# Rotary low parts in one subtraction, high parts copied by ScalarE in portions, and one block of values moved behind the first output products

## The chip, the core and the metric

The kernel runs on one core of a Trainium2 chip. The core has five engines with a queue of instructions each: TensorE (PE, matrix products; PEld is its loading of weights), VectorE (DVE), ScalarE (ACT), GpSimd (POOL) and SyncE (SP, which here only issues DMAs). The metric is the device time of one execution in microseconds, as the median of the runs. Products write PSUM, which has eight banks of 128 partitions by 512 fp32 numbers; all other tiles of the kernel lie in SBUF.

## The reference

One layer: attention with low-rank projections (MLA) over 2048 tokens of width 512, a layer norm, a linear layer, and a second layer norm.

```python
cq = rms_norm(hidden_states @ w_qa.T, q_a_ln_w)               # 384 wide
q = (cq @ w_qb.T)                                             # 16 heads of 192
q_nope, q_pe = (q[..., :128], q[..., 128:])
q_pe = q_pe * cos + rotate_half(q_pe) * sin
ckv = hidden_states @ w_kva.T                                 # 128 + 64 wide
k_pe = k_pe * cos + rotate_half(k_pe) * sin                   # one for all heads
kv = (rms_norm(ckv[..., :128]) @ w_kvb.T)                     # k_nope and v of each head
scores = einsum('bhqd,bhkd->bhqk', q_full, k_full) * scale    # causal
attn = softmax(scores)
out = einsum('bhqk,bhkd->bhqd', attn, v) @ w_o.T
x = layernorm(x + out)
x = layernorm(x + (x @ (weight * scale_weight).T + bias))
```

## The kernel before

**Numbers in two parts.** An operand of a product is held as a high part, rounded to TensorE's fp32r format, and a low part, the remainder. A product is then three products (high by high, high by low, low by high). `split` (L61) makes the two parts: ACT rounds, DVE subtracts.

**Tiles and stages.** The 2048 queries are cut into four blocks of 512 (`b`), the 16 heads into eight pairs (`p`). A block has four query tiles of 128 (`qt`), so that a pair has eight steps in a block (head `j` of query tile `qt`), counted 2 * qt + j from 0 to 7. Block 0 has short rows and runs beside the preparation of keys, values and weights. Blocks 1 to 3 run in `units` (L615) one after the other, with rows up to 1024, 1536 and 2048 keys long. In the trace block 1 runs from about 260 us, block 2 from about 505, block 3 from about 860 to 1332. Then come the output products and both layer norms.

**One step.** `head_scores` (L421) lets PE form the scores of one head and one query tile (L410, products of `Kn` by `qn` and of `Kp` by `pe`), DVE takes the maximum (L448) and makes the bias, ACT takes the exponential (L463, `pr`). `head_probs` (L479) runs a step later: ACT makes the high half of the probabilities (L484, `hl`), DVE the low half (L487), and SP issues the DMA that transposes both into a ring (L491). `values` (L529) multiplies them by V on PE (L540, tile `o`) up to `lag` query tiles later, in two halves; ACT empties `o` into `ot` (L545), and SP stores `ot`.

**PSUM in the blocks.** Two banks (pool `m`) turn among `o`, the projections `ps_qn` and `ps_pe`; a third tile of them waits until the first is emptied by ACT or DVE. The other six banks hold scores. In block 1 they are three tiles of two banks, one tile for each head. In block 2 each head has one tile of two banks and one of one bank, two of each kind. In block 3 each head has two tiles of two banks, and three such tiles turn.

**Projections as fillers.** The queries of the next pair are projected between the steps of this one. `project_nope` (L369) makes `qn` for a pair; `project_pe` (L324) makes `pe`, the rotary part for four heads (a group `g`, two pairs), so it runs at every other pair. Each is a generator, and `fill` (L551) resumes the first of the list `fillers` up to its next `yield`. The tuple `at` in `units` says at which of the eight steps `fill` is called.

`project_pe` has PE form two tiles `ps_pe`, DVE multiplies them by cosine and sine into `prod` (L341), and POOL adds and subtracts, which leaves the rotated numbers in `rp`, 128 partitions by two rows of 512 (L348, L349). ACT rounds them to `ph` (L351). Then the eight pieces of 32 partitions are stacked so that each head has its high parts in partitions 0 to 63 of `pe` and its low parts in 64 to 127. In block 0 and in the first group of block 1 (`quick`), ACT copies the high parts (L360) and DVE, partly POOL, subtracts the low ones. In the other eleven groups POOL does both (L362 and L363).

**Who sets the order.** In blocks 1 to 3 PE and SP follow the program text. ACT, DVE and POOL are ordered by the scheduler of the build, except that from the second query tile of block 3 on ACT and DVE follow the text too (L646). In the text, a head's high and low probabilities stand inside the next head's step, behind that step's first scores.

**The end of the attention.** After the last step two query tiles of values are still to come, `o3_7_2` (15 key tiles, halves of 21 and 24 products) and `o3_7_3`. The loop at L803 mixes the halves of the first with the output products of the first two pairs (`accumulate`, L753, into four PSUM accumulators `accs`, one bank each) and with `value_output` (L173), which multiplies V's weights by the output weights for later pairs. The accumulators take banks that the scores held.

Of the kernel before, what the change touches and what calls it, by code (L numbers as in the profile page):

```python
# [11 lines left out]
F32 = mybir.dt.float32  # L12
F32R = mybir.dt.float32r
AF = mybir.ActivationFunctionType
ALU = mybir.AluOpType
# [4 lines left out]
P = 128  # L20
# [5 lines left out]
NB = 4  # L26
QB = 512
# [22 lines left out]
def mla_block(ctx: ExitStack, tc: tile.TileContext, a, out):  # L50
    nc = tc.nc
# [59 lines left out]
    blk = ctx.enter_context(tc.tile_pool(name="blk", bufs=2, side="right"))  # L111
# [168 lines left out]
    state = {"queue": nc.gpsimd}  # L280
# [43 lines left out]
    def project_pe(b, g, direct=None):  # L324

        if direct is None and ("wpe", b, g) not in state:
            load_wpe(b, g)
        w = state.pop(("wpe", b, g)) if direct is None else direct
        cq, cs = state["cq"], state["cs"]
        prod = prj.tile([P, 2, 2, QB], F32, tag="prod", name=f"prod{b}_{g}")  # L330
        for x in range(2):
            ps = psum["m"].tile([P, QB], F32, tag="m", name=f"ps_pe{b}_{g}_{x}")
            n = 0
            for lt in range(LT):
                for i, k in ((0, 0), (0, 1), (1, 0)):
                    nc.tensor.matmul(  # L336
                        ps, w[:, i, lt, x * P : (x + 1) * P], cq[:, k, lt, :], start=n == 0, stop=n == 8
                    )
                    n += 1
            for k in range(2):  # L340
                nc.vector.tensor_tensor(prod[:, k, x, :], ps, cs[:, k ^ x, :], ALU.mult)  # L341
            if x == 0:
                yield
            elif b or g == 3:
                load_wpe(*((b, g + 1) if g < 3 else (b + 1, 0)))
        rp, tp = prod[:, 0], prod[:, 1]
        eng = nc.vector if (b, g) == (0, 0) else nc.gpsimd
        eng.tensor_tensor(rp[:, 0, :], rp[:, 0, :], rp[:, 1, :], ALU.subtract)  # L348
        eng.tensor_tensor(rp[:, 1, :], tp[:, 0, :], tp[:, 1, :], ALU.add)  # L349
        ph = prj.tile([P, 2, QB], F32R, tag="ph", name=f"ph{b}_{g}")  # L350
        nc.scalar.activation(ph, rp, AF.Copy)  # L351
        pe = blk.tile([P, 4, QB], F32R, tag="pe", name=f"pe{b}_{g}")

        quick = b == 0 or (b, g) == (1, 0)
        for j in range(4):
            q = slice(32 * j, 32 * j + 32)
            for x in range(2):
                to = pe[32 * x : 32 * x + 32, j, :]
                if quick:
                    nc.scalar.activation(to, rp[q, x, :], AF.Copy)  # L360
                else:
                    nc.gpsimd.tensor_copy(to, rp[q, x, :])  # L362
                (nc.gpsimd if not quick or (b, g) == (0, 0) and j % 2 else nc.vector).tensor_tensor(  # L363
                    pe[64 + 32 * x : 96 + 32 * x, j, :], rp[q, x, :], ph[q, x, :].bitcast(F32), ALU.subtract
                )
        state["pe", b, g] = pe
        yield

    def project_nope(b, p, direct=None):  # L369
# [181 lines left out]
    def fill(n=1):  # L551
        while n > 0 and fillers:
            try:
                next(fillers[0])
                n -= 1
            except StopIteration:
                fillers.pop(0)
# [57 lines left out]
    def units(pool, ring, b):  # L615
        lag = min(ring.shape[1] // (2048 * (b + 1)) - 1, 3)

        for p in range(NPAIR):
            put_in(True)


            if p + 1 == NPAIR:
                at = (1, 2, 4, 5) if b < NB - 1 else (1, 3, 5, 7)
            elif p % 2 == 0 and p + 2 < NPAIR:
                at = (0, 1, 2, 3) if (b, p) == (1, 0) else (0, 1, 3, 4)
            else:
                at = (3, 4)
            if b and p % 2 == 0 and p + 2 < NPAIR:
                fillers.append(project_pe(b, p // 2 + 1))
            if p + 1 < NPAIR:  # L630
                fillers.append(project(b, p + 1) if b == 0 else project_nope(b, p + 1))
            elif b + 1 < NB:
                fillers.append(project(b + 1, 0))
            if b == NB - 1 and p == NPAIR - 1:
                ctx_p.close()
                pcr = state["pcr"] = ctx.enter_context(
                    tc.tile_pool(name="pcr", bufs=2, side="right", reuse_waits="tile")
                )
                state["wvo"] = [pcr.tile([P, 2, 2, HID], F32R, name=f"wvo{p}", bufs=1) for p in range(EARLY)]
                for i in range(EARLY):  # L640
                    fillers.append(value_output(i, psum["m"], "m"))
                at = (3, 4, 5, 6)
            for qt in range(4):
                nk = (4 * b + qt + 1) * P
                if (b, p, qt) == (NB - 1, 0, 1):
                    ctx_f.enter_context(tc.manual_schedule(engines={ET.PE, ET.SP, ET.DVE, ET.Activation}))  # L646
                if (b, p, qt) == (0, NPAIR - 1, 3):
                    s0, PT = -4 * nk, prj.tile([P, 4 * nk], F16, tag="ph", name="carry")
                else:
                    s0 = room(2048 * (b + 1), ring.shape[1], 4 * nk, (b, p) == (2, NPAIR - 1) and qt > 0)  # L650
                    PT = ring[:, s0 : s0 + 4 * nk]
                vg = values(b, p, qt, nk, PT)
                if nk <= 512:
                    pi = pair_scores(pool, b, p, qt, nk)
                    flush()
                    probs.append(pair_probs(pool, b, p, qt, nk, PT, *pi))
                    fill()
                    next(side[0], None)
                    if p and qt % 2:
                        next(side[1], None)  # L660
                    if qt % 2:
                        next(side[0], None)
                    run_values(lag)
                    run_values(lag)
                else:
                    for j in range(2):
                        prepare_output(b, p, 2 * qt + j)
                        prev = probs.pop() if probs else iter(())
                        pi = head_scores(pool, b, p, j, qt, nk, prev)
                        probs.append(head_probs(pool, b, p, j, qt, nk, PT, *pi))  # L670
                        if (b, p, qt, j) == (1, 0, 1, 0):
                            half_values()
                            half_values()
                        if 2 * qt + j in at:
                            fill()
                        run_values(lag)
                vals.append([vg, 0, s0, s0 + 4 * nk])
            drain()
        if b:
            flush()  # L680
# [102 lines left out]
    with tc.manual_schedule(engines={ET.PE, ET.SP}), ExitStack() as ctx_f:  # L783
        for b in range(1, NB):
            with ExitStack() as ctx_s:
                for k in ("s", "ts", "us")[b - 1]:
                    psum[k] = ctx_s.enter_context(
                        tc.tile_pool(name=f"ps_{k}{b}", bufs=1, space=PSUM, reuse_waits="tile")
                    )
                pools = [  # L790
                    ctx_s.enter_context(tc.tile_pool(name=f"{k}{b}", bufs=2, reuse_waits="tile")) for k in ("hl", "pr")
                ]
                units(pools, ring, b)

        ps_a = ctx.enter_context(tc.tile_pool(name="ps_a", bufs=4, space=PSUM, reuse_waits="tile"))
        accs = [ps_a.tile([P, HID], F32, tag="acc", name=f"acc0_{t}") for t in range(4)]
        pcq = ctx.enter_context(tc.tile_pool(name="pcq", bufs=1, side="right", reuse_waits="tile"))
        wvo = state["wvo"]
        wvo += [pcq.tile([P, 2, 2, HID], F32R, name=f"wvo{EARLY + i}") for i in range(2)]
        load_wo(2, blk, "pe")  # L800
        latent_load(0, EARLY + 1)
        load_wo(3, blk, "qn")
        for p in range(EARLY):  # L803
            vo = value_output(EARLY + p, psum["m"], "m")
            for t in range(4):
                if len(vals) > 1:
                    half_values()
                accumulate(accs[t], p, t, *cuts[0, p])
                if t in (1 - p, 2 - p):
                    next(vo)  # L810
            cuts[0, EARLY + p] = latent_split(0, EARLY + p)
        while vals:
            half_values()
        put_in(True)
# [160 lines left out]
```

## Time and profile before

| what | value |
|---|---|
| time, median of 3 runs | 1597.79 us (1594.83 to 1601.57) |
| the profiled execution | 1599.18 us, its span 1597.4 us |
| PE matrix products, busy | 1550.6 us, 97% |
| PE idle from 290 to 1332 us | 8.3 us of 1042 |
| PE's longest single wait, at 1337.70 us | 3.56 us, for the DMA that transposes `hl` |
| L463 exponentials, ACT | 324.6 us in 320 |
| L484 high probabilities, ACT | 294.5 us in 320 |
| L487 low probabilities, DVE | 359.4 us in 320 |
| L363 low rotary parts, POOL | 140.4 us in 92, 1526 ns each |
| L362 high rotary parts, POOL | 66.8 us in 88, 760 ns each |
| mean granted TensorE clock | 0.992 of full speed |

The span goes from the first instruction to the last; the profiled execution's own time holds 1.8 us more. A row of the profile names a source line, an engine and an operation, then what it writes and reads, then how many there were and how long one took. "[1.44 <-ACT ot L545]" behind a row of a timeline says that the engine stood idle for 1.44 us before it, and that the eviction of line 545 on ACT ended the wait. An idle engine costs time only if the chain that ends last passes through it.

### The profile page before, as it was taken

The numbers are of one execution on the slowest core, as the hardware profiler recorded it, in microseconds if no ns is written. First come the engines' busy times: TensorE is split into PE (matmuls) and PEld (weight loads), VectorE is DVE, ScalarE is ACT, GpSimd is POOL, SyncE is SP. The second block draws the span as 40 slices with busy tenths as digits, with TensorE's granted clock in tenths as the row PEclk, the third lists the DMA queues.
The fourth block names the chain that finished last, engine by engine and source line by source line (L and its number), as shares of the span: only waits on it lengthen the run. The fifth ranks groups of instructions, "written<-read, shape, count | busy, mean of one in ns | idle before, by whom it ended". The sixth has DMA issues, their size and how long they took to land. (4 is left out here: it accounts for less than half of the span.)

```text
span 1597.4 us, 24700 instructions
## 1 busy us (share of the span) xinstructions
PE 1550.6 (97%) x9130; PEld 1293.8 (81%) x9130; DVE 1164.0 (73%) x2099; ACT 926.1 (58%) x1631; POOL 364.6 (23%) x434
## 2 busy tenths in 40 slices
PE   8898998999999999999999999999999998999997
PEld 7777877888888788888888888888888886788886
DVE  6777777888787878787787777777777775455564
ACT  5767676666665766767765665665666665321120
POOL 2333234252206305050022400400400000022132
PEclk9999999999999999999999999999999999999999
DMA  6888667789897987888896888878678798433230
GB/s 210 255 211 223 173 187 163 163 165 184 166 208 159 180 158 165 164 160 168 154 222 137 165 146 168 157 144 168 137 144 170 155 230 190 145 112 129 92 113 33
DMA packets 633032, 262.49 MB, mean 164 GB/s; under 512 B 570288, under 2 KB 611376, under 8 KB 631888
## 3 DMA queue, kind: packets, MB, share of 16 engines
q1 hardware_dynamic: 621472, 233.62, 68.1%
q0 software_dynamic: 4672, 17.73, 3.6%
q10 hardware_dynamic: 6768, 9.57, 2.1%
q8 instruction: 72, 1.18, 0.3%
q14 instruction: 48, 0.39, 0.1%
HBM read 83.17 MB, written 35.13 MB: 74 GB/s over the span
## 5 line engine op out<-in xcount | busy, mean ns | idle before, releaser
L410 PE MATMUL s<-Kn,qn 128*128 128x512 f32 (+4 forms) x1920 | 519.5, 376 | 6.2 <-ACT pr L463 4.4
L463 ACT ACTIVATE pr<-s,bias,rq 128x1024 f32<-128x1024 f32 (+3 forms) x320 | 324.6, 1018 | 215.0 <-DVE bias L457 157.9
L540 PE MATMUL o<-ring,V 128*128 128x256 f16 x3252 | 395.5, 274 | 12.2 <-DMA ring<-hl 5.2
L487 DVE SCALAR_TENSOR_TENSOR hl<-pr,inv,hl 128x1024 f16<-128x1024 f32 (+7 forms) x320 | 359.4, 1136 | 40.0 <-ACT hl L484 35.2
L410 PEld LDWEIGHTS s<-Kn,qn 128*128 128x128 f32 x1920 | 338.6, 190 | 52.9 <-ACT pr L463 7.8
L540 PEld LDWEIGHTS <-V 128*128 128x128 f16 x3264 | 303.7, 98 | 92.5 <-issue 52.8
L410 PE MATMUL s<-Kp,pe 128*128 128x512 f32 (+4 forms) x1280 | 360.4, 362 | 0.0
L484 ACT ACTIVATE hl<-pr,inv 128x1024 f16<-128x1024 f32 (+7 forms) x320 | 294.5, 961 | 92.6 <-issue 34.4
L448 DVE TENSOR_REDUCE neg<-s 128x1 f32<-128x1024 f32 (+3 forms) x320 | 317.8, 993 | 37.3 <-PE s L410 34.2
L410 PEld LDWEIGHTS s<-Kp,pe 128*128 128x128 f32 x1280 | 233.1, 188 | 29.6
L348 POOL TENSOR_TENSOR prod<-prod 128x512 f32<-128x512 f32 x15 | 19.3, 1288 | 641.9 <-DVE prod L341 641.9
L380 PE MATMUL ps_qn<-cq,wq 128*128 128x512 f32 x576 | 147.0, 400 | 4.1 <-ACT ot L545 3.3
L757 PE MATMUL acc<-wvo,oh 128*128 128x512 f32 x448 | 144.2, 403 | 0.0
L363 POOL TENSOR_TENSOR pe<-prod,ph 32x512 fp32r<-32x512 f32 x92 | 140.4, 1526 | 11.0 <-issue 5.1
L380 PEld LDWEIGHTS ps_qn<-cq,wq 128*128 128x128 f32 x576 | 108.3, 192 | 25.9 <-ACT ot L545 3.9
L757 PEld LDWEIGHTS acc<-wvo,oh 128*128 128x128 f32 x448 | 83.6, 189 | 21.2 <-issue 3.8
L475 DVE TENSOR_SCALAR inv<-sums 128x1 f32<-128x1 f32 x128 | 27.0, 211 | 98.6 <-ACT pr L463 98.5
L757 PE MATMUL acc<-wvo,ol 128*128 128x512 f32 x224 | 88.2, 394 | 0.0
L336 PE MATMUL ps_pe<-cq,wpe 128*128 128x512 f32 x288 | 71.9, 395 | 1.5 <-DMA cq<-cq_d 1.4
L545 ACT ACTIVATE ot<-o 128x256 f32<-128x256 f32 x128 | 48.4, 379 | 40.9 <-PE o L540 37.1
L362 POOL CAST pe<-prod 32x512 fp32r<-32x512 f32 x88 | 66.8, 760 | 3.3
L64 ACT ACTIVATE oh<-o 128x1024 fp32r<-128x1024 f32 x28 | 29.7, 1061 | 65.1 <-PE acc L757 51.8
(140 smaller groups left out, 1586.1 us busy)
## 6 DMA issues: line engine op xcount, KB each, us to landing
wq<-wq_d SPq DMA_DIRECT2D x22, 768.0 KB, 5.7
o<-ot_d SPq DMA_DIRECT2D x32, 512.0 KB, 3.3
ot_d<-ot SPq DMA_DIRECT2D x97, 128.0 KB, 2.3
wpe<-wpe_d SPq DMA_DIRECT2D x10, 768.0 KB, 5.4
wq<-wq_d POOLq DMA_DIRECT2D x9, 768.0 KB, 6.4
wq_d<-wst SPq DMA_DIRECT2D x9, 512.0 KB, 4.4
cq_d<-cqst SPq DMA_DIRECT2D x18, 256.0 KB, 3.5
wo<-in_wo_dram SPq DMA_DIRECT2D x4, 1024.0 KB, 6.2
```

The lines of the kernel that those rows point to most:

```text
L336: nc.tensor.matmul(ps, w[:, i, lt, x * P : (x + 1) * P], cq[:, k, lt, :], start=n == 0, stop=n == 8)
L362: nc.gpsimd.tensor_copy(to, rp[q, x, :])
L363: (nc.gpsimd if not quick or (b, g) == (0, 0) and j % 2 else nc.vector).tensor_tensor(pe[64 + 32 * x : 96 + 32 * x, j, :], rp[q, x, :], ph ...
L380: nc.tensor.matmul(ps, w[:, i, lt, j * P : (j + 1) * P], cq[:, k, lt, :], start=n == 0, stop=n == 8)
L410: nc.tensor.matmul(ps[:, :w], lhs, K[:, i, c0 : c0 + w], start=n == 0, stop=n == 4)
L448: nc.vector.tensor_reduce(neg[:, ti : ti + 1], v, axis=AX.XY, op=ALU.max, negate=True)
L463: nc.scalar.activation(pr[:, c0 : c0 + n * w].rearrange("p (a c) -> p a c", a=n), v, AF.Exp, bias=bias, scale=r, accum_out=sums[:, ti : ti ...
L484: nc.scalar.activation(hl[:, 0, c], pr[:, c], AF.Copy, scale=inv)
L487: nc.vector.scalar_tensor_tensor(hl[:, 1, c], pr[:, c], inv, hl[:, 0, c], ALU.mult, ALU.subtract)
L540: nc.tensor.matmul(ps[:, :256], vt[:, i, k % 4, :], v[:, :, l, k, :], start=n == 0, stop=n == 3 * kts - 1)
L545: nc.scalar.activation(ot, ps[:, :256], AF.Copy)
L757: nc.tensor.matmul(acc, l[:, t, c], state["wvo"][p][:, i, j, :], start=p == 0 and j == 0 and n == 0, stop=p == NPAIR - 1 and j == 1 and n ...
```

## The change

It has three parts.

1. In the eleven groups that are not `quick`, the eight subtractions of 32 partitions on POOL become one of 128 partitions by 1024 numbers, from `rp` and `ph` into the second half of `prod` (`pl`), and POOL copies the eight low pieces from there. The eight high pieces are copied by ACT.
2. The group's work is issued in more steps: a `yield` stands ahead of `ph`, and the copies are a generator of their own (`stack`), which yields after the first and the third of its four pieces and goes to the end of `fillers`. The tuples `at` have seven entries in place of four, so that PE's projections come at the same steps as before, `ph` and the first two high copies one step later than before, and the other high copies at the last two entries.
3. At the end, the first half of `o3_7_2` is issued behind all of the first pair's output products, and its second half behind the first tile of the second pair's; the steps of `value_output` move with them.

```diff
         rp, tp = prod[:, 0], prod[:, 1]
+        quick = b == 0 or (b, g) == (1, 0)
         eng = nc.vector if (b, g) == (0, 0) else nc.gpsimd
         eng.tensor_tensor(rp[:, 0, :], rp[:, 0, :], rp[:, 1, :], ALU.subtract)
         eng.tensor_tensor(rp[:, 1, :], tp[:, 0, :], tp[:, 1, :], ALU.add)
+        if not quick:
+            yield
         ph = prj.tile([P, 2, QB], F32R, tag="ph", name=f"ph{b}_{g}")
         nc.scalar.activation(ph, rp, AF.Copy)
-        pe = blk.tile([P, 4, QB], F32R, tag="pe", name=f"pe{b}_{g}")
-
-        quick = b == 0 or (b, g) == (1, 0)
-        for j in range(4):
-            q = slice(32 * j, 32 * j + 32)
-            for x in range(2):
-                to = pe[32 * x : 32 * x + 32, j, :]
-                if quick:
-                    nc.scalar.activation(to, rp[q, x, :], AF.Copy)
-                else:
-                    nc.gpsimd.tensor_copy(to, rp[q, x, :])
-                (nc.gpsimd if not quick or (b, g) == (0, 0) and j % 2 else nc.vector).tensor_tensor(
-                    pe[64 + 32 * x : 96 + 32 * x, j, :], rp[q, x, :], ph[q, x, :].bitcast(F32), ALU.subtract
-                )
-        state["pe", b, g] = pe
+        pe = state["pe", b, g] = blk.tile([P, 4, QB], F32R, tag="pe", name=f"pe{b}_{g}")
+
+        if not quick:
+            pl = tp.bitcast(F32R)
+            nc.gpsimd.tensor_tensor(pl, rp, ph.bitcast(F32), ALU.subtract)
+
+        def stack():
+            for j in range(4):
+                q = slice(32 * j, 32 * j + 32)
+                for x in range(2):
+                    hi, lo = pe[32 * x : 32 * x + 32, j, :], pe[64 + 32 * x : 96 + 32 * x, j, :]
+                    nc.scalar.activation(hi, rp[q, x, :], AF.Copy)
+                    if not quick:
+                        nc.gpsimd.tensor_copy(lo, pl[q, x, :])
+                    else:
+                        (nc.gpsimd if (b, g) == (0, 0) and j % 2 else nc.vector).tensor_tensor(
+                            lo, rp[q, x, :], ph[q, x, :].bitcast(F32), ALU.subtract
+                        )
+                if not quick and j in (0, 2):
+                    yield
+
+        rest = stack()
+        if quick:
+            for _ in rest:
+                pass
+        else:
+            next(rest)
+            fillers.append(rest)
         yield
...
             if p + 1 == NPAIR:
-                at = (1, 2, 4, 5) if b < NB - 1 else (1, 3, 5, 7)
+                at = (1, 2, 3, 4, 5, 6, 7) if b < NB - 1 else (1, 3, 5, 7)
             elif p % 2 == 0 and p + 2 < NPAIR:
-                at = (0, 1, 2, 3) if (b, p) == (1, 0) else (0, 1, 3, 4)
+                at = (0, 1, 1, 2, 3, 4, 5) if (b, p) == (1, 0) else (0, 1, 2, 3, 4, 5, 6)
             else:
                 at = (3, 4)
...
-                        if 2 * qt + j in at:
-                            fill()
+                        fill(at.count(2 * qt + j))
                         run_values(lag)
...
         for p in range(EARLY):
             vo = value_output(EARLY + p, psum["m"], "m")
             for t in range(4):
-                if len(vals) > 1:
+                if p and len(vals) > 1:
                     half_values()
                 accumulate(accs[t], p, t, *cuts[0, p])
-                if t in (1 - p, 2 - p):
+                if t in (1, 2):
                     next(vo)
```

## The prediction

> **What bounds the kernel now.** I read the busy shares first, then the busy time by stretch, then what TensorE waited for inside the attention blocks, then the timelines around each of those waits.
>
> ```profile
> PE 1550.6 (97%) x9130; PEld 1293.8 (81%) x9130; DVE 1164.0 (73%) x2099; ACT 926.1 (58%) x1631; POOL 364.6 (23%) x434
> ```
>
> ```profile
> 290.00:560.00 270.00, 264.83 (x1614) 223.81 (x1612) 221.28 (x458) 174.26 (x285) 83.11 (x73) 1.00 0.88 176
> 560.00:900.00 340.00, 338.89 (x2068) 285.06 (x2067) 271.58 (x494) 226.00 (x400) 83.92 (x72) 1.00 0.82 165
> 900.00:1332.00 432.00, 429.96 (x2622) 356.54 (x2621) 323.54 (x465) 275.18 (x404) 42.84 (x36) 1.00 0.81 161
> ```
>
> The columns are stretch, length, then busy time of PE, weight loads, DVE, ACT and POOL. From 290 to 1332 us PE lacks only 5.2 + 1.1 + 2.0 = 8.3 us. The change leaves PE's own order untouched up to there (it only renumbers which fill step issues a projection), so a gain inside the attention blocks is capped at that, while a loss is not: any wait put on PE goes straight to the end. Nearly all the idle time lies beside a rotary group, at 293.6 (0.58), 296.1 (0.52), 489.2 (0.71), 499.8 (0.63), 526.4 (1.44), 530.0 (1.20), 878.2 (0.92), 884.9 (0.19), 1004.3 (0.38) and 1124.2 us (0.38). I call the eleven changed groups by block and number, (1,1) to (3,3).
>
> **POOL's part.** Per group POOL does two adds of 1.29 us, eight casts (about 6.4 us) and eight subtractions (about 12.6 us).
>
> ```profile
> L363 POOL TENSOR_TENSOR pe<-prod,ph x92: 1262/1294/2115, 44.7 to 1135.9; 32x512 fp32r<-32x512 f32 x92
> L362 POOL CAST pe<-prod x88: 602/609/1475, 272.3 to 1124.3; 32x512 fp32r<-32x512 f32 x88
> L360 ACT ACTIVATE pe<-prod x40: 612/628/633, 41.0 to 255.7; 32x512 fp32r<-32x512 f32 x40
> ```
>
> After: one subtraction of 128x1024. A POOL pass over 512 elements takes 1.29 us on 128 partitions (the adds) as on 32, so 2.6 us; then eight low copies, 6.4 us, as the casts now. POOL falls by 12.6 - 2.6 = 10 us a group. That is worth nothing by itself: PE waits for POOL nowhere in its list, and a group is read a pair later or more. Bounds: zero and zero, even if the subtraction took twice as long.
>
> It helps DVE, which POOL slows. The low half of a probability row, 128x640, with POOL idle and during POOL's subtractions (two of them):
>
> ```profile
> 358.56 0.89 DVE L487 SCALAR_TENSOR_TENSOR hl<-pr,inv,hl 128x640 f16<-128x640 f32 x1
> 524.27 3.73 DVE L487 SCALAR_TENSOR_TENSOR hl<-pr,inv,hl 128x640 f16<-128x640 f32 x2 [2.10 <-ACT hl L484]
> ```
>
> 0.89 against 1.87 us each. The Trainium skill ("SBUF — State Buffer", Who interferes with whom) speaks against a wide instruction here: a VectorE instruction with two SBUF inputs and a GpSimd one that reads SBUF share a port, whichever starts first holds it for the whole instruction, and the other is blocked. By the rule one 2.6 us subtraction can hold one DVE instruction for 2.6 us instead of 1.3. By the row, about five such DVE instructions a group lose 1 us each. Either way DVE loses at most 2.6 us at once, then only the smaller loss beside copies (1.34 us in place of 0.89 at 329.7), so DVE gains some 2 us a group. This ends waits that DVE causes: I take 0.6 of the 1.10 at (1,1), the 0.63 at (2,0) and the 1.20 at (2,1); in block 3 the late ph moves a head on, which ends 0.19 + 0.38 + 0.38 = 0.95. The 0.92 at 878.2 stays: that head's ACT waited for a transpose.
>
> **ACT's part: blocks 1 and 2.** Eight high copies per group at 0.64 us (four in a row take 2.56 in block 0) add 5.1 us to ACT. The fill steps would spread them over later heads, but in blocks 1 and 2 the scheduler orders ACT itself: in the built program all eight stand around ph, as four, ph, four, with at most a probability row between. ACT runs in order, so exponentials and evictions queue behind 6.1 us where 1.06 stood. Each group is replayed with the durations of its rows, overlaps of about 0.1 us taken off. Group (1,2):
>
> ```profile
> 327.75 1.29 POOL L348 TENSOR_TENSOR prod<-prod 128x512 f32<-128x512 f32 x1 [36.78 <-DVE prod L341]
> 331.40 0.98 ACT L463 ACTIVATE pr<-s,bias,rq 128x768 f32<-128x768 f32 x1
> 336.01 0.38 ACT L545 ACTIVATE ot<-o 128x256 f32<-128x256 f32 x1
> 336.39 2.23 PE L380 MATMUL ps_qn<-cq,wq 128*128 128x512 f32 x9
> ```
>
> ps_qn takes the PSUM buffer that ot empties, with no slack: 336.01 + 0.38. After: the copies can begin at 329.0 (first POOL add done), 331.6, row 332.3, ph 333.3, copies 335.9, exponential 336.8, qn 337.4, exponential 338.4, ot 338.8. PE waits **2.4 us**. (1,3) is the same picture with the row ahead: ot at 398.6, wanted at 396.44, **2.2**. (3,0): the copies start at 829.05 behind the exponentials; +5.1 +1.0, row 836.6, exponentials 838.3, ot 838.7, wanted at 836.88 by the next o: **1.8**. (2,0): ps_qn waits for DVE's qn, which comes 1.2 us late instead of 0.71: +0.5, less the 0.63, **-0.1**. (2,1): the exponential of the next head but one now ends at 523.6 and its score buffer was wanted at 521.51, a wait of 2.2 where 2.64 stood, **-0.4**. (1,1) **-0.6**. (2,2), (2,3): ot at 615.0 against 615.8 wanted: **0**. Sum **+5.3**; bounds -3.6 (all waits of before but the DMA one gone, no new one) and +10 (each of the eight pays 1.2 more than the mean).
>
> **ACT's part: block 3.** ACT and DVE stand in program order, so the portions do land later: ph and two copies, then four, then two. The first finds room (projection heads). The last two fall in the longest rows, where a loop runs with almost no slack: exponential, high half on ACT, low half on DVE, maximum, bias, next exponential.
>
> ```profile
> 1028.93 2.08 ACT L484 ACTIVATE hl<-pr,inv 128x960 f16<-128x960 f32 x2 [0.26 <-ACT ot L545]
> 1030.06 1.22 DVE L487 SCALAR_TENSOR_TENSOR hl<-pr,inv,hl 128x960 f16<-128x960 f32 x1
> 1032.82 1.21 ACT L463 ACTIVATE pr<-s,bias,rq 128x1024 f32<-128x1024 f32 x1 [1.80 <-DVE bias L457]
> 1035.51 0.86 PE L410 MATMUL s<-Kn,qn 128*128 128x512 f32 x3
> ```
>
> The first of ACT's two halves ends near 1030.0, DVE starts on it at once, and PE's scores at 1035.51 need the buffer of the exponential that ends at 1034.03: 1.4 us of slack. Four copies put this hl off by 2.56 less about 0.3 of waiting it hides: 2.2. Two more before the next row: 1.28 - 0.53, in all 2.95. The third head has 0.6 of slack (exponential to 1048.0, scores at 1048.72), so PE loses 2.95 - 0.6 = **2.3 us** a group; 3 x 2.3 = 6.9, less the 0.95 above: **+5.9**. Bounds -1.0 (slack I don't see) and +8.
>
> **The end.** Before, PE reached the values last but one at 1334.14 and waited for their transpose:
>
> ```profile
> 1337.70 3.60 PE L540 MATMUL o<-ring,V 128*128 128x256 f16 x21 [3.56 <-DMA ring<-hl]
> 1340.94 1.20 PE L757 MATMUL acc<-wvo,oh 128*128 128x512 f32 x2
> ```
>
> ```profile
> 1338.00:1342.00 4.00, 4.00 (x23) 3.11 (x22) 2.27 (x4) 2.86 (x5) 0.00 (x0) 0.60 1.06 200
> ```
>
> The granted clock is 0.60 behind it: 21 products take 3.24 us (2.22 at 1023.8), the six of acc 2.08 (1.39 later); so 3.56 + 1.7. After, the first pair's products stand first. The PSUM addresses of the build put accumulator 0 in the buffer freed by the exponential at 1330.3, but 1 and 2 in that of the last head's first exponential, 1335.92 + 1.21. So six products (1.39) run, then PE waits from 1335.53 to 1337.26: 1.73. Then wo products and the rest; the values want DVE's low half of wo, behind the last rows until 1343.3: 0.2. Saved 5.26 - 1.93 = **3.3 us**. Is PE cold after 1.73? The skill ("TensorE: Matmul & The Clock Gate", Part 1) has the clock halve after an idle window of about 3.4 us; the row at 526.40 shows nine products at 2.36 us behind an idle 1.44. By both warm; by the one cold row, 1.6. On SP one load of o now goes ahead of a 128 KB store; that store is late with its values and nobody at hand waits for it. Bounds 1.5 to 3.6.
>
> **Sum.** +5.3 + 5.9 - 3.3 = +7.9 us on the profiled execution's 1599.18 (span 1597.4), which is 1.4 above the median of the runs. On the median: 1597.8 + 7.9 = **1605.7**.
>
> **Rivals.** *Relief wins (faster):* the scores and evictions turn out to have 2 us more slack than I read, no copy reaches PE, and 6.0 us of the old waits go too, with 3.3 at the end: 1588.5; with half the waits, 1592. For it: ACT is busy 64% of blocks 1 to 3. Against it: ps_qn at 336.39 starts the moment its buffer is free. It decides if ot in (1,2) is ready by its old time. *ACT becomes the bound:* every block 1 and 2 group stops PE by most of its 5.1 us less 2 of slack: 8 x 3.1 + 5.9 - 3.3 = +27, 1625. For it: the block of 6.1 us is longer than the slack of any head replayed. Against: (2,2) and (2,3) have 0.8 to spare after all of it. *Blocks 1 and 2 as read, block 3 with slack:* 5.3 - 1.0 - 3.3 = +1, 1599. *The spreading is not done* in blocks 1 and 2 is not a rival but part of the forecast.
>
> **How the numbers follow.** 0.5% is 8 us, what a measurement of this kernel can tell from none. My case (+3 to +12) 0.66; block 3 with slack (-1 to +3) 0.10; relief wins 0.13; ACT the bound 0.11. My case lies across the line: half of it over 8. Slower 0.33 + 0.11 = 0.44; faster 0.06 (less than half of the relief case reaches 8); same 0.50. Low end: the sum of the low bounds, -3.6 - 1.0 - 3.3, is -8; I stop at -3. High end +14, into the third case.
>
> **What would show it.** ACT's rows of 32x512: 128 in place of 40, near 0.63. PE waits for ot near 336 and 396, for exponentials in the long rows of block 3 (2.3 a group), and 1.7 in place of 3.56 at 1334, at full clock. DVE rows near 524 under 1.4 us. PE's idle time from 290 to 1332 near 19 us; if below 8, ACT had slack that I didn't see and the forecast is wrong.

## The result, and the profile after

The changed kernel takes 1619.12 us, the median of 4 runs (1617.41 to 1624.14), against 1598.01 for the kernel before in the same runs: a ratio of 1.0132 with a 95% interval of 1.0102 to 1.0161. It is slower by 21.1 us, where 7.9 were forecast, and lies outside the range of 1595 to 1612. The profiled execution is the slowest of the four: 1624.14 us, span 1622.4, 25.0 above the profiled execution of before.

The first part of the page, busy time of each engine:

```profile
PE 1559.7 (96%) x9130; PEld 1297.7 (80%) x9130; DVE 1143.7 (70%) x2099; ACT 978.1 (60%) x1719; POOL 253.5 (16%) x357
```

POOL lost 111 us and ACT gained 52, as the change says. TensorE does the same 9130 products, yet is busy 9.1 us longer: part of the loss is not idle time. The same three stretches as before, at the times at which the same products now run (columns as before; the last but two is the granted clock):

```profile
295.00:576.00 281.00, 269.30 (x1618) 226.72 (x1618) 215.14 (x458) 193.39 (x317) 43.85 (x44) 0.99 0.86 171
576.00:920.00 344.00, 339.95 (x2065) 285.79 (x2065) 263.09 (x496) 242.22 (x428) 41.96 (x44) 1.00 0.82 163
920.00:1359.00 439.00, 431.84 (x2624) 356.34 (x2622) 319.46 (x465) 288.41 (x423) 22.73 (x22) 1.00 0.80 158
```

PE's idle time in them is 11.7 + 4.1 + 7.2 = 22.9 us (8.3 before, 19 forecast), and its busy time rose by 7.4. The rows that replace those of the subtractions, by shape:

```profile
L366 ACT ACTIVATE pe<-prod 32x512 fp32r<-32x512 f32 x128 | 80.4, 628 | 4.7 <-POOL prod L349 2.8 <-DVE prod L349 0.3
L368 POOL CAST pe<-prod 32x512 fp32r<-32x512 f32 x88 | 62.9, 714 | 4.6
...
L359 POOL TENSOR_TENSOR prod<-prod,ph 128x1024 fp32r<-128x1024 f32 x11 | 26.3, 2391 | 44.7 <-ACT ph L354 41.3 <-PE s L426 3.4
```

A copy takes 0.63 us and the wide subtraction 2.39, as priced (0.64 and 2.6).

**Where the time went.** PE issues the same products in the same order in all kernels here, but for the first part of the tail. So the n-th product's start in one trace, less its start in the trace of before, says how late a kernel is at that place, and the growth of this lateness over a stage is the stage's cost. Stages are named by their rotary group and by the times of before. The kernels of the columns from "high copies on POOL" on are explained below.

| stage, us of before | forecast | changed | changed, again | high copies on POOL | wide alone | wide, one edge | copies spread | fastest |
|---|---|---|---|---|---|---|---|---|
| (1,1), 285 to 305 | -0.6 | 4.5 | 6.0 | -1.5 | -1.5 | -1.5 | 3.0 | -1.5 |
| (1,2), to 370 | 2.4 | 1.6 | 1.6 | 0.0 | 0.0 | 0.0 | 1.1 | 0.0 |
| (1,3), to 426 | 2.2 | 2.5 | 2.5 | 0.0 | 0.0 | 0.0 | 1.1 | 0.0 |
| (2,0), to 484 | -0.1 | -0.3 | -0.3 | 0.5 | 0.3 | -0.1 | -0.2 | 0.4 |
| (2,1), to 579 | -0.4 | 2.7 | 2.6 | 6.3 | 7.1 | 2.9 | 5.5 | -0.7 |
| (2,2), (2,3), to 825 | 0 | 0.0 | 0.0 | 0.0 | 0.0 | 0.0 | 0.0 | 0.0 |
| (3,0), to 850 | 1.8 | 2.0 | 2.0 | 0.0 | 0.0 | 0.0 | 2.0 | 0.0 |
| first heads of block 3, to 909 | none | 2.7 | 0.9 | 5.9 | 6.3 | -0.8 | 3.4 | -1.6 |
| (3,1) to (3,3), to 1187 | 5.9 | 6.9 | 7.6 | -1.5 | -0.1 | -0.1 | 7.0 | -1.5 |
| the end, 1333 to 1380 | -3.3 | -2.4 | -2.3 | -2.4 | 1.0 | -0.1 | -2.3 | -2.4 |

With a few tenths between, the changed kernel's sum from 285 us on is 20.3. The rest of its 25.0 is 4.6 us that stand before that point, in block 0, which the change does not touch.

### The profile page after: what moved, and what is told of

Read it like the earlier page. It is cut to its first block, busy times and chain, and to the rows that moved or that the text cites. A ratio compares the mean times of both kernels' runs of the same rounds, so it can differ in the third digit from the quotient of the medians.

```text
span 1622.4 us, 24734 instructions
## 1 busy us (share of the span) xinstructions
PE 1559.7 (96%) x9130; PEld 1297.7 (80%) x9130; DVE 1143.7 (70%) x2099; ACT 978.1 (60%) x1719; POOL 253.5 (16%) x357
## 5 line engine op out<-in xcount | busy, mean ns | idle before, releaser
L426 PE MATMUL s<-Kn,qn 128*128 128x512 f32 (+4 forms) x1920 | 523.5, 378 | 15.9 <-ACT pr L479 12.7
L426 PEld LDWEIGHTS s<-Kn,qn 128*128 128x128 f32 x1920 | 340.4, 191 | 65.7 <-ACT pr L479 20.3
L503 DVE SCALAR_TENSOR_TENSOR hl<-pr,inv,hl 128x1024 f16<-128x1024 f32 (+7 forms) x320 | 338.5, 1070 | 44.0 <-ACT hl L500 41.0
L366 ACT ACTIVATE pe<-prod 32x512 fp32r<-32x512 f32 x128 | 80.4, 628 | 4.7 <-POOL prod L349 2.8
L65 DVE TENSOR_TENSOR ol<-o,oh 128x1024 fp32r<-128x1024 f32 x28 | 38.8, 1386 | 38.7 <-ACT oh L64 38.7
```

What stands on the lines that cost most here:

```text
L65: nc.vector.tensor_tensor(l, ps, h.bitcast(F32), ALU.subtract)
L366: nc.scalar.activation(hi, rp[q, x, :], AF.Copy)
L426: nc.tensor.matmul(ps[:, :w], lhs, K[:, i, c0 : c0 + w], start=n == 0, stop=n == 4)
L503: nc.vector.scalar_tensor_tensor(hl[:, 1, c], pr[:, c], inv, hl[:, 0, c], ALU.mult, ALU.subtract)
```

## The experiments

All kernels compute the same numbers. Times stand beside those of the kernel before in the same runs; the ratios compare all runs of both and can differ a little from the quotient of the two medians. The theory I began with (A) was that ScalarE's load in the rotary groups makes the loss; its rivals are named in the expectations.

**The end alone, and what block 0 does by itself.** The edit is the third part of the change, in the kernel before.

```diff
-                if len(vals) > 1:
+                if p and len(vals) > 1:
                     half_values()
                 accumulate(accs[t], p, t, *cuts[0, p])
-                if t in (1 - p, 2 - p):
+                if t in (1, 2):
```

> The kernel before with the change at the end alone (first pair's output products ahead of the values last but one). Theory A (the loss of the change sits in the rotary groups, the end is a gain): TensorE's 3.56 us wait at 1334 and the cold stretch behind it go, about 1.8 for an accumulator's bank comes, so 2.5 us faster than before (1595.5), as the end of the changed kernel's profile showed; nothing moves up to 1330 us. Rival B (the end's gain exists only because the changed kernel arrives there late): no gain, 1598 or more. Block 0 is that of both kernels: if the 4.6 us that the changed kernel's profile was later at the end of block 0 were chance, block 0 ends here near 240.6, as before.

1595.98 against 1597.2, ratio 0.9987 (0.9979 to 0.9995). The trace gains 2.4 us at the end and nothing elsewhere. The waits there, in its timeline:

```profile
1336.45 0.73 PE L757 MATMUL acc<-wvo,oh 128*128 128x512 f32 x2 [1.75 <-ACT pr L463]
...
1343.39 2.45 PE L540 MATMUL o<-ring,V 128*128 128x256 f16 x21 [0.79 <-DVE wvo L68]
```

1.75 was forecast as 1.73; 0.79 as 0.2. The 21 products behind take 2.45, not the 3.60 of before, so the clock stays up. Rival B falls. Block 0 ends 1.0 us earlier than before here. Whether the 4.6 us are the change's, a second trace of the changed kernel shows.

> The changed kernel itself, once more, for its time beside the run with the turned buffer (1618.7) and for a second trace. Theory: 1617 to 1622; blocks 1 to 3 and the end within a few tenths of a us of the first trace (13 us lost up to 860, 9.6 in block 3, 2.5 gained at the end), while the end of block 0, 4.6 us late in the first trace, varies.

1618.41 against 1597.36, ratio 1.0135 (1.0114 to 1.0155). Its profiled execution took 1615.39 us and is 4.3 us early where the first was 4.6 late; from there on it loses 20.5 us, the first 20.3. So the 4.6 are not the change's, and the 8.8 us between these two executions are block 0's. The stages repeat within a few tenths, but for the first, in which the slow clock behind one wait lasts longer (below), the start of block 3, where it falls in one trace only, and 0.7 us in block 3.

**High copies back on POOL.** Everything else of the change stays.

```diff
-                    nc.scalar.activation(hi, rp[q, x, :], AF.Copy)
+                    if quick:
+                        nc.scalar.activation(hi, rp[q, x, :], AF.Copy)
+                    else:
+                        nc.gpsimd.tensor_copy(hi, rp[q, x, :])
```

> The changed kernel, but the eight high copies of each changed group stand on POOL again; wide subtraction, later ph, fill steps and end stay. Theory A (ScalarE's 5.1 us per group, in order ahead of exponentials and evictions, makes the loss): nearly all of the 20 us goes, 1595 to 1599. Rival C (the later ph and the new fill steps make it, since they move the group a head on): at least 15 us stay, 1613 or more. Rival D (where block 3's first probability row lies on the last row of block 2 still being transposed): of it alone 2 to 3 us stay, in the first heads of block 3.

1605.35 against 1597.2, ratio 1.0056 (1.0037 to 1.0074): between the two, and the table says why. At (1,1), (1,2), (1,3), (3,0) and in all of block 3's groups the loss is gone, and there are gains of 1.5 at (1,1) and 0.7 in two groups of block 3. So theory A is shown for those stages, and rival C (the later steps) is refuted: the later `ph` is a gain. But two stages lose some 6 us each, of which the changed kernel loses a part.

**The wide subtraction alone.** In the kernel before, the subtraction becomes wide and the low pieces are copied; the copies of high parts stay on POOL, `ph` where it was, and the end too.

> The kernel before with the wide subtraction alone: one of 128x1024 and eight low copies in place of eight subtractions, high copies on POOL, no later step, end as before. Theory A: POOL falls by some 3.7 us per group net, VectorE gains a little, TensorE's waits near 490 to 530 shrink by up to 2 us: 1596 to 1598. Rival E (the wide subtraction holds the port it shares with VectorE for 2.4 us at once): up to 1 us more per group, 1605 to 1609. Rival D: the build of this one also puts block 3's first probability row on the last row of block 2, so if that alone makes the wait at the start of block 3, it shows 2 to 3 us here too (about 1599).

1611.28 against 1597.2, ratio 1.008 (1.0058 to 1.0103): above even rival E's figure. But it isn't spread over the groups, as E wants it; it sits in the same two stages. Its timeline at the first:

```profile
509.66 1.44 ACT L489 ACTIVATE hl<-pr,inv 128x576 f16<-128x576 f32 x2 [2.79 <-DMA ring<-hl]
510.47 0.82 DVE L492 SCALAR_TENSOR_TENSOR hl<-pr,inv,hl 128x576 f16<-128x576 f32 x1 [3.15 <-ACT hl L489]
...
513.00 1.28 DVE L341 TENSOR_TENSOR prod<-ps_pe,cs 128x512 f32<-128x512 f32 x2
...
514.33 4.21 PE L336 MATMUL ps_pe<-cq,wpe 128*128 128x512 f32 x9 [7.88 <-DVE prod L341]
```

(`state["first"]` below is the second of the products `prod` of (2,1)'s first tile.) Block 2's first row `hl` waits for a transpose that still reads its buffer. The build put DVE's low half of that row ahead of the products of (2,1), which could have begun at 502.8, when the first `ps_pe` was done; PE needs their PSUM bank. In the kernel before, those products stood first:

```profile
507.35 0.68 DVE L341 TENSOR_TENSOR prod<-ps_pe,cs 128x512 f32<-128x512 f32 x1
507.95 0.95 DVE L448 TENSOR_REDUCE neg<-s 128x1 f32<-128x768 f32 x1
...
512.25 0.82 DVE L487 SCALAR_TENSOR_TENSOR hl<-pr,inv,hl 128x576 f16<-128x576 f32 x1 [1.61 <-ACT hl L484]
```

Nothing in the text asks for the new order; the scheduler of the build chose it (why, no run shows). So one edge was added that forbids it (theory F), the same instructions otherwise:

```diff
+            low = nc.vector.scalar_tensor_tensor(hl[:, 1, c], pr[:, c], inv, hl[:, 0, c], ALU.mult, ALU.subtract)
+            if (b, p, qt, j) == (2, 0, 0, 0):
...
+                    tc.add_manual_dep(low.ins, state["first"].ins.name,
...
```

> The kernel with the wide subtraction alone took 1611.3: its trace loses some 6.4 us net at 514, where VectorE's products of group (2,1) stand behind low halves that wait for transposes, and 6.2 us net at 878, where block 3's first row lies on block 2's last. Here the scheduler is told by one edge to put those products ahead of the low halves; with it the build also has the buffers of the kernel before. Theory F (the wide subtraction costs nothing itself; what it costs is the order that the scheduler makes of the shorter POOL work): both losses go, 1594 to 1598. Rival E (a wide instruction holds the port): it stays above 1605.

1599.53 against 1598.18, ratio 1.0006 (0.9996 to 1.0015). The loss is gone to within the noise, 1.5 us above the range of F, and E falls. That the two engines hold each other up is seen all the same, in DVE's and POOL's timelines:

```profile
458.20 1.14 DVE L496 SCALAR_TENSOR_TENSOR hl<-pr,inv,hl 128x896 f16<-128x896 f32 x1
...
487.37 2.42 DVE L496 SCALAR_TENSOR_TENSOR hl<-pr,inv,hl 128x896 f16<-128x896 f32 x1
...
485.85 2.98 POOL L361 TENSOR_TENSOR prod<-prod,ph 128x1024 fp32r<-128x1024 f32 x1
```

At 458.2 POOL is idle; at 487.4 the same operation takes 1.28 us longer. In eight of the eleven groups a low half that starts under the wide subtraction ends only after it: 1.59 to 2.42 us, where it takes 0.89 (128x640, kernel before) or 1.14 (128x896) with POOL idle. That agrees with the rule of the Trainium skill that I weighed ("SBUF — State Buffer", Who interferes with whom). It costs PE nothing where it can be told apart: the stages (2,2), (2,3) and (3,0) have such a low half each and cost 0.0. F promised too much in one point: the stage of (2,1) still costs 2.9, since the products now stand behind a sum of exponentials and the maxima of the next head (PE waits 4.08 us for them at 510.97); whether the longer low half at 487 has a few tenths in it stays open.

**A row's buffer at the start of block 3.** With the edge, the second loss went too. It is another effect of order. Rows lie in two pools, for `pr` and for `hl`, which are opened anew for each block; the `hl` pool of block 2 has four buffers and hands out the one that comes free first. By the addresses in the builds, which no trace shows, the last row of block 2 got the buffer on which block 3's first `pr` lies in the changed kernel and in the wide subtraction alone; in the kernel before, the last but one got it. In the changed kernel's timeline ACT then stands still until that row is transposed:

```profile
886.63 1.20 ACT L479 ACTIVATE pr<-s,bias,rq 128x1024 f32<-128x1024 f32 x1 [7.18 <-DMA ring<-hl]
...
887.98 0.71 PE L426 MATMUL s<-Kn,qn 128*128 128x320 f32 x3 [2.02 <-ACT pr L479]
```

Two kernels move that first row elsewhere and leave the order of blocks 1 to 3 as it was: one opens block 3's two pools in the other order, one takes an unused tile from the pool of `pr` first.

```diff
-                    ctx_s.enter_context(tc.tile_pool(name=f"{k}{b}", bufs=2, reuse_waits="tile")) for k in ("hl", "pr")
-                ]
+                    ctx_s.enter_context(tc.tile_pool(name=f"{k}{b}", bufs=2, reuse_waits="tile")) for k in ("hl", "pr")[:: -1 if b == NB - 1 else 1]
+                ][:: -1 if b == NB - 1 else 1]
```

> The changed kernel with block 3's two row pools in the other order, so that its first probability row lies on a row that was transposed earlier. Rival D (the 2.02 us wait at 888 and its cold stretch, 2.7 us in all, come from that buffer): they go, 1616.4. Theory A alone (the row is late because ScalarE is late): nothing changes, 1619. The end of the kernel may move by a fraction of a us, since wvo lies where these pools were.

```diff
+                if b == NB - 1:
+                    turn = pools[1].tile([P, 2048], F32, tag="pr", name="turn")
+                    nc.gpsimd.memset(turn[:, :1], 0.0)
                 units(pools, ring, b)
```

> The changed kernel with one unused tile taken first from block 3's pool of rows, so that its first row lies where block 2's last rows were computed, not where one is still being transposed; nothing at the end changes place. Rival D: the 2.02 us wait at 888, its cold stretch and the 1.1 us that stood in the kernel before go, about 3.9 less: 1615.2. If the row is late for ScalarE's load alone: 1619.

In both traces the stage falls to -1.1 (2.7 and 0.9 in the two traces of the changed kernel), and of the waits of 0.22 and 2.02 only the first is left:

```profile
870.86 0.71 PE L426 MATMUL s<-Kn,qn 128*128 128x320 f32 x3 [0.23 <-ACT pr L479]
```

Rival D is shown by the traces. The times do not show it. With the pools swapped it is 1625.78 against 1597.2 (1.0163, 1.0142 to 1.0183): PE waits 8.1 us at the end for an output weight `wvo`, which by the addresses now lies on rows that are transposed last; I had allowed a fraction of a us. With the unused tile it is 1618.66 against 1598.18 (1.0128, 1.0108 to 1.0148): its trace loses 17.6 us from 285 us on, against 20.3 and 20.5, but the runs (1614.58 to 1621.24) scatter by more than that.

**Are the copies too much, or too much at once?** In blocks 1 and 2 the scheduler put all eight copies around `ph`. First, ACT was made to follow the text in blocks 1 and 2, as it does in block 3.

```diff
-                units(pools, ring, b)
+                with tc.manual_schedule(engines={ET.Activation}) if b < NB - 1 else ExitStack():
+                    units(pools, ring, b)
```

> The changed kernel with ScalarE in program order in blocks 1 and 2 too, so that the eight high copies do land in portions of two, four and two, a head apart, as in block 3. Theory G (the block of 6.1 us at once makes the loss of blocks 1 and 2, 13 us): most of it goes, 8 to 11 us less, 1608 to 1611. Rival H (it is ScalarE's 5.1 us per group, however spread, or program order puts other rows late): less than 3 us gained, or slower, 1616 or more.

1634.5 against 1598.18, ratio 1.023 (1.0215 to 1.0246). The loss of blocks 1 and 2 is spread over pairs with groups and without, and PE's list of waits from 270 to 1400 us (total, times, longest) begins so:

```profile
PE s L426 <- ACT pr L479: 17.7, 20, 2.9
PE ps_qn L396 <- ACT ot L561: 12.4, 11, 1.9
```

In the changed kernel the same two rows say 12.7 us in 12 times and 2.3 in one. Most of what is new is evictions (`ot`), eleven times. So this run tells of the text's order of all rows, not of the copies. The next one ties only `ph` and the copies, each behind the exponential that stands before it in the text (`state["exp"]`), and the copies behind `ph` (`behind`):

```diff
+                    high = nc.scalar.activation(hi, rp[q, x, :], AF.Copy)
+                    if not quick and b < NB - 1:
+                        for it in (behind, state["exp"]):
+                            tc.add_manual_dep(high.ins, it.ins.name,
...
```

> The changed kernel with ScalarE's order left to the scheduler in blocks 1 and 2, but each portion of high copies tied by edges behind ph and behind the exponential that stands before it in the program: two, four and two copies, a head or more apart, nothing else ordered by hand. It separates the spreading from the program order of all rows, which the run with ScalarE in program order mixed up (36 us slower than before). Theory G: the waits of (1,1) to (2,1), 10.5 us, fall to under 4; 1611 to 1614. Rival H (ScalarE has no room for 5.1 us more per group in these heads, however spread): 1618 or more.

1615.7 against 1597.36, ratio 1.0121 (1.0101 to 1.0141). Block 1 gains (5.1 lost in place of 8.6 and 10.1), and (2,1) gives it back. Its timeline there, portions of (2,0) and (2,1):

```profile
503.30 2.55 ACT L368 ACTIVATE pe<-prod 32x512 fp32r<-32x512 f32 x4
...
507.63 0.79 PE L431 MATMUL s<-Kn,qn 128*128 128x384 f32 x3 [2.27 <-ACT pr L484]
...
558.72 0.79 PE L431 MATMUL s<-Kn,qn 128*128 128x384 f32 x3 [1.87 <-ACT pr L484]
```

At 507.63 four copies ahead of an exponential are enough to stop PE; at 558.72 it is two (1.27 us at 552.45), with four halves and an eviction behind them. Blocks 1 and 2 lose 10.5 us up to 579, against 11.0 and 12.4, and the time lies between the ranges of both theories. In block 1 theory G is right in part: spreading takes off 3.5 to 5.0 us. At (2,1) these portions find no room, as rival H has it. Whether other places or portions of one copy would fit was not tried.

**The parts that gain, together.** High copies on POOL, wide subtraction, later `ph` and the new end, with the edge for (2,1):

> The changed kernel with the high copies back on POOL took 1605.4; here with the same edge as in the run above. Its ledger without the two order losses: 1.4 gained at (1,1), 3 of the waits at 526 and 530, 1 to 1.6 at 878, 2 in block 3 by the later ph, 2 at the end. Theory A with F: 1588 to 1592, faster than before. Rival C (the later steps cost by themselves): not under 1597.

1594.94 against 1598.18, ratio 0.9979 (0.9968 to 0.999): faster than before, so rival C falls, but 3 us above the range that I had given. Every stage is near what was expected but (2,1), which loses 3.0; there the products still stand behind a sum of exponentials:

```profile
508.38 1.28 DVE L341 TENSOR_TENSOR prod<-ps_pe,cs 128x512 f32<-128x512 f32 x2
...
509.71 3.92 PE L336 MATMUL ps_pe<-cq,wpe 128*128 128x512 f32 x9 [4.05 <-DVE prod L341]
```

Two more kernels add to this one: they put the products ahead of that sum (the first edge here), and then ahead of the next head's maxima and mask too (the second, and one like it for the mask).

```diff
+                tc.add_manual_dep(state["total"].ins, last.ins.name,
...
+            if (b, p, qt, j) == (2, 0, 0, 1) and "first" in state:
+                tc.add_manual_dep(top.ins, state["first"].ins.name,
...
```

> The kernel with high copies on POOL, wide subtraction, later ph, the new end and the edge that puts VectorE's products of (2,1) ahead of the first low halves (1594.9), with one more edge: ahead of that row's sum of exponentials too, for which they still waited (TensorE 4.05 us at 509.7). If that order is all that stands there, some 4 us less: 1590 to 1592; if something else is late at that place, 1594 to 1596.

> The kernel of the run before (1593.3) with the products of (2,1) put ahead of the next head's maxima and mask as well, the order that VectorE had there in the kernel before. In its trace TensorE still waited 2.49 us for them at 509.5 and the stage from 484 to 579 us cost 1.4 net. If that wait is the order's, the stage gains 2 to 3 us like the other late waits there and the whole takes 1589 to 1591; if the products then put a maximum or a low half late, the time stays at 1593.

They take 1593.34 against 1597.36 (0.9974, 0.9961 to 0.9987) and 1590.49 against 1597.81 (0.9959, 0.9946 to 0.9973). The first gained less than expected, since 2.49 us of the wait went over to the maxima; the second is the fastest here, 7.3 us under the kernel before. In its windows over the same three stretches PE lacks 3.8 + 0.0 + 1.4 us:

```profile
287.00:556.00 269.00, 265.22 (x1619) 224.43 (x1619) 218.86 (x457) 174.50 (x285) 70.43 (x76) 1.00 0.88 178
556.00:894.00 338.00, 338.00 (x2067) 284.91 (x2066) 269.97 (x494) 225.98 (x400) 71.19 (x76) 1.00 0.82 165
894.00:1325.00 431.00, 429.59 (x2625) 357.05 (x2624) 324.29 (x465) 275.21 (x404) 35.64 (x39) 1.00 0.82 161
```

## Why the prediction was wrong

The signs of the three parts (blocks 1 and 2, block 3, the end) were right, and so were most of the waits that I worked out. The sum is short by 12.4 us (7.9 against 20.3 from 285 us on), and four steps make up 11.9 of it.

**The group (1,1): -0.6 forecast, 4.5 and 6.0 measured.** This is the step that failed most. I gave this group only DVE's relief and did not replay ACT's block of 6.1 us in it; in the others I followed what it puts off only as far as exponentials and evictions. The changed kernel's timeline shows the rest of the way:

```profile
276.40 2.54 ACT L366 ACTIVATE pe<-prod 32x512 fp32r<-32x512 f32 x4
...
280.31 2.56 ACT L366 ACTIVATE pe<-prod 32x512 fp32r<-32x512 f32 x4
282.89 0.99 ACT L479 ACTIVATE pr<-s,bias,rq 128x768 f32<-128x768 f32 x1
...
287.47 1.39 DVE L503 SCALAR_TENSOR_TENSOR hl<-pr,inv,hl 128x768 f16<-128x768 f32 x1
...
288.89 1.42 SPq L507 DMA_TRANSPOSE ring<-hl  x1
...
298.53 1.80 PE L556 MATMUL o<-ring,V 128*128 128x256 f16 x9 [4.09 <-DMA ring<-hl]
```

The same exponential and low half in the kernel before:

```profile
273.37 0.97 ACT L463 ACTIVATE pr<-s,bias,rq 128x768 f32<-128x768 f32 x1
...
275.95 1.01 DVE L487 SCALAR_TENSOR_TENSOR hl<-pr,inv,hl 128x768 f16<-128x768 f32 x1
```

The low half comes 11.5 us later; less block 0's 4.6 it is 6.9 us late; SP, which works in order, issues its transpose late and all behind it, and the values that are due find nothing in the ring. Behind the wait the granted clock is 0.50 from 299 to 302 us, which costs another 1.6. In the second trace the wait is 4.45 and the slow stretch behind it costs 2.7; that is the difference between 4.5 and 6.0. The relief itself came: with the copies on POOL the stage gains 1.5.

**The group (2,1): -0.4 forecast, 2.7 and 2.6 measured.** What I worked out is there, and better than forecast: the product that stood at 521.51 before waits 1.29 us behind the copies (forecast 2.2), and the 2.64 us of before are gone. The loss comes from another wait, 2.30 us, that stands ahead of these copies; that it is about as long as the 2.2 of the forecast is chance:

```profile
524.26 1.44 ACT L500 ACTIVATE hl<-pr,inv 128x576 f16<-128x576 f32 x2 [2.37 <-DMA ring<-hl]
525.07 0.82 DVE L503 SCALAR_TENSOR_TENSOR hl<-pr,inv,hl 128x576 f16<-128x576 f32 x1 [2.74 <-ACT hl L500]
525.80 0.95 DVE L464 TENSOR_REDUCE neg<-s 128x1 f32<-128x768 f32 x1
...
529.69 0.99 ACT L479 ACTIVATE pr<-s,bias,rq 128x768 f32<-128x768 f32 x1 [3.72 <-DVE bias L473]
530.83 1.55 PE L426 MATMUL s<-Kn,qn 128*128 128x512 f32 x3 [2.30 <-ACT pr L479]
531.32 2.53 ACT L366 ACTIVATE pe<-prod 32x512 fp32r<-32x512 f32 x4
...
540.22 0.96 PE L426 MATMUL s<-Kn,qn 128*128 128x512 f32 x3 [1.29 <-ACT pr L479]
```

It is the order of DVE again, as with the wide subtraction alone: the low half of block 2's first row, which waits for a transpose, now stands ahead of the next head's maximum; in the kernel before the maximum stood first (507.95, the low half at 512.25). So bias, exponential and PE are late before the first copy runs. No run forbids that order alone in the changed kernel; but in the build with the copies spread the maximum is first again (515.73, the low half at 518.53), and the same product waits 0.41. Behind the 2.30 the clock falls:

```profile
530.80:534.30 3.50, 3.47 (x8) 2.72 (x9) 1.15 (x5) 3.44 (x7) 0.85 (x1) 0.52 0.89 266
...
890.00:893.40 3.40, 3.40 (x11) 2.43 (x11) 3.06 (x3) 1.18 (x2) 0.00 (x0) 0.59 0.00 0
```

The granted clock is 0.52 behind this wait and 0.59 behind the 2.02 us at 887.98 (second row). The two stretches cost 1.6 and 1.7 us, and I had priced none of the new waits in the blocks with one.

**The start of block 3: not in the forecast, 2.7 and 0.9 measured.** I had taken the 0.92 us at 878 to stay. What the change does there goes through the order in which buffers of rows are handed out, which the build shows and I did not look at: I read PSUM addresses for the end, but not those of SBUF for the rows.

**Block 3: 5.9 forecast, 6.9 and 7.6 measured.** The mechanism is as described, four and then two copies in the longest rows, and the size nearly so. The wait comes as two, one for each of the two heads:

```profile
928.69 2.56 ACT L366 ACTIVATE pe<-prod 32x512 fp32r<-32x512 f32 x4
...
936.91 0.96 PE L426 MATMUL s<-Kn,qn 128*128 128x512 f32 x3 [0.98 <-ACT pr L479]
...
945.05 0.70 PE L426 MATMUL s<-Kn,qn 128*128 128x320 f32 x3 [0.90 <-ACT pr L479]
```

**What held.** (1,3) and (3,0) came as forecast (2.2 and 2.5, 1.8 and 2.0), (2,2) and (2,3) have room; (1,2) was 1.6 for 2.4, and its wait (0.91 at 347.06) is for `qn` on DVE, not for the eviction that I had named. POOL's relief is worth nothing by itself, and the scheduler undoes the spreading, both as read. The end gained 2.4 of 3.3: the bank's wait is right to 0.02 us, and DVE's `wvo` is 0.6 us later than I had it. The rival in which ACT becomes the bound gave 1625 by a uniform loss in every group of blocks 1 and 2; the time came near to it, the uniform loss did not. I gave it 0.11, and the range stopped short of it. Of my upper bounds, +8 held the groups of block 3. The +10 for blocks 1 and 2 did not (13.0 and 14.3 measured, to 850 us), and it was a slip: eight times 1.2 above a sum of 5.3 is 14.9.

## What to carry to other kernels

Where work is added to an engine that runs in order, follow the late instruction through everything behind it, to the DMA queue that transposes or stores its result, and not only to the first buffer that PE needs; and price a wait of two microseconds on TensorE with the slow clock behind it (1.5 to 1.7 us here, in 13 of 17 cases). Where a scheduler or a pool decides order and buffers, compare the two builds' order on every engine near the first use of each buffer: taking 3 us a group from POOL, for which PE never waited, cost 12 us by order, and one edge took that back. Undo one part at a time and compare by stage: the total hid that the other parts of this change, with DVE's order set by hand at one place, are worth 7 us of gain.

## What the runs showed of the hardware

**The clock falls behind shorter waits than I had taken.** I rested on the Trainium skill ("TensorE: Matmul & The Clock Gate", Part 1), by which an idle window of about 3.4 us halves the clock. In all fourteen traces, blocks 1 to 3: behind 24 waits of 1.20 to 1.84 us the granted clock stays at 1.00; behind 13 of 17 waits of 1.87 to 2.93 us it falls to 0.50 for some 3 us, and the next products lose 1.5 to 1.7 us together; behind all ten of 4.05 us and more they lose 1.3 to 2.9. The four exceptions are the one wait of 2.25 us at (1,3), in four traces. So here the measurement differs from the page. The page also calls that window free-running, which may be why; no run here shows it. The two traces of the changed kernel differ by this at the start of block 3: a wait of 2.02 us with the slow clock behind it in the one, 1.84 without in the other.

**Block 0 varies by itself.** In thirteen traces of kernels with the same block 0, PE reaches 285 us of before between 4.3 us early and 4.6 late. In the late trace ACT waits 5.71 us at 59 us for DMAs that store prepared weights, but in the trace of the end alone, which is 1.0 us early, it waits 5.33 there; what makes the difference stays open. A difference of 2 or 3 us in later stages needs the trace by stage, or more runs than four.
